# Cross-attention with a scan: features dealt four to a partition, and two steps of the order written later

## The chip, the cores and the metric

The kernel runs on one core of one Trainium2 chip. The time is what the device takes for one execution, in microseconds (us); of several runs the median is given. Every figure of the profile comes from one profiled execution of the kernel.

## The reference

For one sequence of T = 4096 queries and S2 = 3202 context rows, both with H = 512 features, all in float32 (the batch is 1; `input_ids` is not used):

```python
x = layernorm(builder_state, g1, beta1)          # 4096 x 512
base_n = layernorm(base_state, g1, beta1)        # 3202 x 512
q, k, v = heads(x, Wq, bq), heads(base_n, Wk, bk), heads(base_n, Wv, bv)   # 8 heads of 64
attn = softmax(q @ k.T / sqrt(64))
x = builder_state + (attn @ v) @ W_o.T + b_o
xn = layernorm(x, g2, beta2)
U = (xn @ W_in.T + b_in) @ Bmat                  # 4096 x 64
def step(s, u_t):                                # one after the other over t
    s = silu(s @ A.T) + u_t
    return (s, s)
states = scan(step, 0, U)
out = x + states @ Cmat + (program_probs.mean(axis=1) @ W_prog.T + b_prog)
```

## The kernel before

**Three parts.** Up to about 215 us the context is normalised in chunks, transposed by TensorE, and multiplied by Wk and Wv; both results are stored in device memory (`kd`, `vd`). From there to about 1960 us runs the attention. What is left then, the end of the scan, the last rows and the output, is written at the end.

**The attention.** The queries go in 8 blocks of 512. A block has 4 pairs of heads and each pair 2 halves of 256 queries, which makes 8 units. A unit has 13 steps over the keys. A step is `scores` on TensorE (L635, two score tiles that take turns), `weights` on ScalarE (L705, the exponential) and `product` on TensorE (L745). The weights of a unit are summed step by step (`add`, L713): on VectorE (DVE), and for steps 2, 6 and 10 on GpSimd (POOL). At the unit's end GpSimd adds the two halves of the sum (`fold`, L720), TensorE sums over the partitions (`sums`, L763, tile pd), ScalarE copies the denominators (L797), VectorE inverts and scales, and `fall` (L807) keeps a sum of them. The keys and values of each step are loaded on SyncE's queue (L1098, L1106).

**Between the steps** of a block stand two other chains.

- `queries`, for the block that comes next, in two halves of 256 rows: x is loaded (L880), VectorE takes each row's mean and variance (`stats`, L845), GpSimd makes from them a factor and a shift in three small operations (`factors`, L849 to L851), and ScalarE applies them (`scaled`, L857). VectorE transposes 32 by 32 (`flip`, L932), and SyncE issues 16 DMAs a half (`move`, L944), which bring the 32 by 32 blocks to their partitions, in the tile xn with the features across the partitions. From it TensorE makes the queries of each pair of heads (`heads`, L312).
- `project`, for a block that is done: the residual rows xr are loaded (L978), GpSimd adds the output bias (`row`, L981), TensorE multiplies the attention's output by Wo (`outs`, L987, tile pa), VectorE adds the two (`x1`, L1000), GpSimd adds the last term (`mod`, L1004), and the rows are stored for the end (L1007). The same rows are normalised, flipped and moved as above, and TensorE makes the scan's inputs of them (`inputs`, L1042, tile pu), which ScalarE stores (`kept`, L1051).

The first block's queries, those of the last block and the last block's rows are transposed by TensorE instead (L283); the function `mixes(Q)` tells which.

**The order** of the instructions of the attention is written ahead by `Plan` (L71 on): each piece has an engine, a cost in ns, a due time, pieces that it comes after and buffers that it takes. A list scheduler goes through time with these costs and gives each engine that falls free the ready piece with the earliest due time. Due times count in `STEP`s of 2150 ns, one for each key step; d is the time around which a chain is placed. `from_(d)` names the scores of the step at time d, as something to come after. The chip knows nothing of these times: each engine runs its list in order, and waits where a piece needs another engine's.

```python
plan.add((*k, "scaled"), "ACT", 800, partial(scaled_, v, gets[t], t),
         [(*k, "factors")] + ([(*ks[0], "scaled")] if t else []), d + 3 * STEP + t,
         [] if t else ["xh", "xh"], [("fs", (*k, "stats"))] + gives[t : t + 1])
```

**Layout before.** Partition p of xn holds the features p, 128 + p, 256 + p and 384 + p. A move brings to each of its 32 partitions four pieces of 64 elements, which lie apart in xn.

Of the kernel before, what the change touches and what calls it, by code (L numbers as in the profile page):

```python
# [20 lines left out]
P = 128  # L21
# [149 lines left out]
def xattn_ssm_kernel(  # L171
# [49 lines left out]
    g2s = const.tile([P, NC], F32, name="g2s")  # L221
    be2s = const.tile([P, NC], F32, name="be2s")
    bqkv = const.tile([P, 3 * NC], F32, name="bqkv")
    wc = const.tile([P, NC, NS], F32, name="wc")
# [52 lines left out]

    def transposes(pool, tag, xh, n, name):

        name = f"tp_{name}"  # L280
        tp = pool.tile([P, NC, P], F32, tag=tag, name=name) if pool else m_tile([P, NC, P], name)
        for c in range(NC):
            nc.tensor.transpose(  # L283
                tp[:, c, :n], xh[:n, c * P : (c + 1) * P], ident[:n, :n]
            )
        return tp[:, :, :n]
# [15 lines left out]
    def turned(xn, xh, t, name):  # L302

        tp = transposes(None, "m", xh, P, name)
        yield
        nc.scalar.copy(xn[:, :, t * P : (t + 1) * P], tp)

    def heads(Q, hp, xn):

        pq = m_tile([P, 512], f"pq_{Q}_{hp}")  # L310
        for i in range(NC):
            nc.tensor.matmul(  # L312
                pq,
                wq[:, i, hp * P : (hp + 1) * P],
                xn[:, i, :],
                start=(i == 0),
                stop=(i == NC - 1),
            )
# [9 lines left out]
    def first_queries(x0):  # L328

        xn = first_xn["xn"] = xnp.tile([P, NC, QB], F32, tag="xn", name="xn_0")  # L330
        for t in range(NT):
# [30 lines left out]
    def fetch_w(k, queue, part=slice(0, NC)):  # L362
        queue.dma_start(raw[k][:, part], wsrc[:, part, k * H : (k + 1) * H])

    def gain(k, w):
        for i in range(NC):
            nc.vector.tensor_scalar(
                w[:, i, :], raw[k][:, i, :], g1s[:, i : i + 1], None, ALU.mult
            )
# [9 lines left out]
    def shift(k):  # L379

        t = weighted(raw[k], be1s, f"shift_{k}")
        yield
# [16 lines left out]
    def side():  # L399
# [43 lines left out]
        for i in range(NC):  # L443
            nc.tensor.matmul(
                pt[:, i, :NS], wct[:, i * P : (i + 1) * P], twice, start=True, stop=True
            )
# [61 lines left out]
    def norm_chunk(c):  # L508
        if c < NCH:
            xhs[c] = normalize(cxs.pop(c), keys(c), f"c{c}", pool=cin)  # L510

    def turn_chunk(c):
        if c < NCH:
            g, n = c // GC, keys(c)
            if c % GC == 0:
                cts[g] = ctp.tile([P, NC, GC * CK], F32, tag="ct", name=f"ct_{g}")
            o = key0(c) - key0(g * GC)
            copy = nc.vector.tensor_copy if c % 2 else nc.scalar.copy
            copy(cts[g][:, :, o : o + n], transposes(kps, "t", xhs.pop(c), n, f"c{c}"))  # L519

    with tc.manual_schedule():
# [264 lines left out]
    def finish(w, i, d, plan):  # L786
# [22 lines left out]
        def scale(part):  # L809
# [14 lines left out]
        for t, part in enumerate(parts):  # L824
# [4 lines left out]
                     [("rd", ("den", i, 0))])  # L829
        plan.add(("fall", i), "DVE", 340, fall, [("inverse", i, t) for t in range(len(parts))],  # L830
                 d + 9000, [], [("rd", ("den", i, 0))])
# [4 lines left out]

    def norm_pieces(plan, ks, gets, d, after, names, gives):

# [20 lines left out]
        for t, (k, v) in enumerate(zip(ks, vs)):  # L859
            plan.add((*k, "stats"), "DVE", 870, partial(stats_, v, gets[t], names[t]), [after[t]],  # L860
                     d + t, ["fs"])
            plan.add((*k, "factors"), "POOL", 1050, partial(factors_, v), [(*k, "stats")], d + 2000)
            plan.add((*k, "scaled"), "ACT", 800, partial(scaled_, v, gets[t], t),
                     [(*k, "factors")] + ([(*ks[0], "scaled")] if t else []), d + 3 * STEP + t,
                     [] if t else ["xh", "xh"], [("fs", (*k, "stats"))] + gives[t : t + 1])
        return vs

    def queries(plan, Q, d):
# [3 lines left out]
        for half in range(2):  # L872
# [9 lines left out]
            for t in range(2):  # L882
                plan.add((*ks[t], "load"), "SP", 800, partial(load, t),
                         [(*ks[0], "load")] if t else [from_(d - 2 * STEP)], d - 2 * STEP + t, [] if t else ["x"])
            free = ("x", (*ks[0], "load"))
            nv = norm_pieces(plan, ks, [lambda t=t, v=v: v["x"][:, t] for t in range(2)], d,
                             [(*k, "load") for k in ks], [f"x{r}" for r in at],
                             [] if mixes(Q) else [free] * 2)

            def open_(half=half):  # L890
                if half == 0:
                    w["xn"] = xnp.tile([P, NC, QB], F32, tag="xn", name=f"xn_{Q}")

            def move_(a, half=half, v=v, open_=open_):
                if a == 0:
                    open_()
                move(w["xn"][:, :, half * QU : (half + 1) * QU], v["x"], a)

            def turn(half=half, nv=nv, at=at, v=v, open_=open_):
                open_()  # L900
                xn = w["xn"][:, :, half * QU : (half + 1) * QU]
                v["turns"] = [turned(xn, nv[t]["xh"], t, f"x{at[t]}") for t in range(2)]
# [5 lines left out]
            if mixes(Q):  # L908
# [21 lines left out]
    def flip(pair, xh, t):  # L930

        nc.vector.transpose(  # L932
            pair.rearrange("p t h -> p (t h)").rearrange("p (g t r) -> p t g r", t=2, r=TB)[:, t],
            xh.rearrange("p (g r) -> p g r", r=TB),
        )

    def move(xn, pair, a):

        n = 2 * TB
        of = pair[a * TB : (a + 1) * TB].rearrange("p t h -> p (t h)").rearrange(  # L940
            "p (c b k) -> p b c k", b=P // TB, k=n
        )
        for b in range(P // TB):
            nc.sync.dma_start(xn[b * TB : (b + 1) * TB, :, a * n : (a + 1) * n], of[:, b])  # L944

# [19 lines left out]
    def project(plan, Q, halves, d, index):  # L965

        for half in halves:
# [49 lines left out]
            for t in range(2):  # L1017
# [20 lines left out]
            def inputs(w=w, at=at, last=last):  # L1038
                w["pu"] = m_tile([P, P], f"pu_{at[0]}")
                for c in range(NC):  # L1040
                    for t in range(2):
                        nc.tensor.matmul(  # L1042
                            w["pu"][t * NS : (t + 1) * NS], wc[:, c, :],
                            w["xn"][:, t, c, :] if last else mixed(w["xn"][:, c, :], t),
                            start=(c == 0), stop=(c == NC - 1), skip_group_check=True,
# [21 lines left out]
            else:  # L1067
                copied, xn2, after = [], (*ks[0], "move0"), 16

                def move_(a, w=w, at=at):  # L1070
                    if a == 0:
                        w["xn"] = xp_.tile([P, NC, QU], F32, tag="xn2", name=f"xn2_{at[0]}", bufs=1)
                    move(w["xn"], w["x1"], a)
# [5 lines left out]
                for a in range(P // TB):  # L1079
                    plan.add((*ks[0], f"move{a}"), "SP", 2600, partial(move_, a),  # L1080
                             [(*k, "flip") for k in ks] + ([xn2] if a else []), d + (6 + 2 * a) * STEP,
                             [] if a else ["xn2"], [("x1", (*k2, "outs"))])
# [254 lines left out]
    def last_rows(plan, d):  # L1337
# [26 lines left out]
        def turn_(g):  # L1364
            if g:
                tp = v["tp"][g] = sv["pyl"].rearrange("p (c k) -> p c k", c=NC)
                for c in range(NC):
                    nc.tensor.transpose(tp[:, c, :], v["xh"][g][:, c * P : (c + 1) * P], ident)
            else:
# [106 lines left out]
    def unit(plan, i):  # L1476
# [30 lines left out]
        for c in range(NDC):  # L1507
# [25 lines left out]
            if c == 1:  # L1533
                plan.add(("rest", i), "DVE", 700, partial(rest, w), [("add", i, 1), ("extra", first)],
                         d + 1300, [], [("extra", ("extra", first))])
# [103 lines left out]
    def attend():  # L1639
# [31 lines left out]
        def turned_():  # L1671
# [6 lines left out]
            for c in range(NC):  # L1678
                cs = slice(c * P, (c + 1) * P)
                nc.tensor.transpose(banks[0][:, cs], xh[:, cs], ident)  # L1680
            nc.scalar.copy(xn, banks[0].rearrange("p (c k) -> p c k", c=NC))
# [204 lines left out]
```

## Time and profile before

| | |
|---|---|
| Time, median of 3 runs | 2033.97 us (2031.74 to 2038.98) |
| Profiled execution: its time, its span | 2036.71 us, 2034.9 us |
| Mean granted clock of TensorE | 0.988 of full speed |
| Busy: TensorE, its weight loads | 1967.0 us (97%), 1258.4 us (62%) |
| Busy: VectorE, ScalarE, GpSimd | 1210.8 us (60%), 1134.3 us (56%), 796.7 us (39%) |
| DMA | 246,935 packets, 204.28 MB |

PE is TensorE, PEld its weight loads, DVE VectorE, ACT ScalarE, POOL GpSimd, SP SyncE and SPq what it issues. A line such as L635 is one of the kernel before. A row of a timeline gives the start in us, the duration in us, engine, line, operation, the tiles written and read, and the number of instructions that it joins; in brackets stand the idle time before it and what ended that. A row of a table of windows gives the stretch and its length, then busy time and number of instructions for PE, PEld, DVE, ACT and POOL, then TensorE's granted clock as a share of full speed, the share of the DMA engines that was busy, and GB/s. A row of the waits gives who waited for whom, the total in us, how often, and the longest. A row that groups a line's instructions gives their number, the shortest, median and longest duration in ns, and the first and last start.

### The profile page before, as it was taken

The numbers are of one execution on the slowest core, as the hardware profiler recorded it, in microseconds if no ns is written. First come the engines' busy times: TensorE is split into PE (matmuls) and PEld (weight loads), VectorE is DVE, ScalarE is ACT, GpSimd is POOL, SyncE is SP. The second block draws the span as 40 slices with busy tenths as digits, with TensorE's granted clock in tenths as the row PEclk, the third lists the DMA queues.
The fourth block names the chain that finished last, engine by engine and source line by source line (L and its number), as shares of the span: only waits on it lengthen the run. The fifth ranks groups of instructions, "written<-read, shape, count | busy, mean of one in ns | idle before, by whom it ended". The sixth has DMA issues, their size and how long they took to land.

```text
span 2034.9 us, 66527 instructions
## 1 busy us (share of the span) xinstructions
PE 1967.0 (97%) x29070; PEld 1258.4 (62%) x29070; DVE 1210.8 (60%) x1533; ACT 1134.3 (56%) x1478; POOL 796.7 (39%) x631
## 2 busy tenths in 40 slices
PE   8999999999999999999999999999999999989996
PEld 4444566665666666666666566666666666655674
DVE  4321367566766666666656675677556655655585
ACT  2233566665656555555666665656565565654553
POOL 2111234345433453345334643345334533444324
PEclk9999999999999999999999999999999999999998
DMA  5632333223422343224322342233322322544475
GB/s 170 188 102 64 100 95 90 59 80 93 110 71 77 92 110 87 76 69 110 90 63 81 83 108 65 80 105 102 83 77 77 93 75 63 149 139 116 123 201 197
DMA packets 246935, 204.28 MB, mean 100 GB/s; under 512 B 80809, under 2 KB 220073, under 8 KB 246637
## 3 DMA queue, kind: packets, MB, share of 16 engines
q1 hardware_dynamic: 242088, 192.28, 33.4%
q10 hardware_dynamic: 4548, 7.67, 1.3%
q8 instruction: 231, 3.78, 0.8%
q14 instruction: 68, 0.55, 0.1%
HBM read 156.32 MB, written 29.88 MB: 92 GB/s over the span
## 4 chain that ended last, share of the span: by engine, by line
PE 70%; DVE 11%; POOL 9%; issue 3%; SPq 3%; ACT 2%; DMA 2%; DVEq 0%; POOLq 0%; ACTq 0%
PE s L635 24%; PE po L745 24%; DVE acc L713 7%; PE pq L312 5%; POOL acc L713 4%; PE pk L584 4%; PE pv L551 4%; PE pa L987 3%; SPq L944 2%; ACT p L705 1%; PE pd L763 1%; DVE rd L804 1%; DMA x<-in_x_dram 1%; POOL rstd_x L850 1%; DVE acc L699 1%
## 5 line engine op out<-in xcount | busy, mean ns | idle before, releaser
L705 ACT ACTIVATE p<-s,shifts 128x1024 f32<-128x1024 f32 (+1 forms) x832 | 889.1, 1080 | 528.5 <-PE s L635 517.4
L635 PE MATMUL s<-q,k 64*64 64x256 f32 x12800 | 839.8, 379 | 16.7 <-ACT p L705 15.6
L713 DVE TENSOR_TENSOR acc<-p,acc 128x1024 f32<-128x1024 f32 (+1 forms) x515 | 620.2, 1204 | 381.4 <-POOL acc L713 315.7
L745 PE MATMUL po<-p,v 64*64 64x256 f32 x12800 | 825.1, 378 | 0.0
L713 POOL TENSOR_TENSOR acc<-p,acc 128x1024 f32<-128x1024 f32 x189 | 446.7, 2363 | 765.4 <-DVE acc L713 419.6
L635 PEld LDWEIGHTS s<-q,k 64*64 64x64 f32 x12800 | 485.9, 134 | 248.1 <-ACT p L705 36.5
L745 PEld LDWEIGHTS po<-p,v 64*64 64x64 f32 x12800 | 491.4, 134 | 192.8 <-issue 6.1
L720 POOL TENSOR_TENSOR acc<-acc 128x512 f32<-128x512 f32 x64 | 102.1, 1595 | 141.1 <-DVE acc L713 141.1
L713 DVE TENSOR_TENSOR acc<-p,p 128x1024 f32<-128x1024 f32 x64 | 95.9, 1499 | 40.0 <-ACT p L705 34.3
L312 PE MATMUL pq<-xn,wq 128*128 128x512 f32 x256 | 118.3, 605 | 0.0
L804 DVE RECIPROCAL rd<-rd 128x256 f32<-128x256 f32 (+1 forms) x65 | 112.4, 1729 | 2.2
L987 PE MATMUL pa<-wo,o 128*128 128x512 f32 x240 | 107.0, 599 | 0.0
L551 PE MATMUL pv<-wv,ct 128*128 128x512 f32 (+1 forms) x208 | 96.4, 617 | 1.0 <-ACT ct L519 0.7
L584 PE MATMUL pk<-ct,wk 128*128 128x512 f32 (+1 forms) x224 | 88.8, 549 | 0.0
L784 DVE TENSOR_TENSOR o<-po,o 128x256 f32<-128x256 f32 x64 | 27.1, 423 | 95.3 <-ACT o L780 94.8
L312 PEld LDWEIGHTS pq<-xn,wq 128*128 128x128 f32 x256 | 46.0, 189 | 57.5 <-issue 57.5
L321 ACT ACTIVATE q<-pq,bias 128x512 f32<-128x512 f32 x32 | 22.0, 687 | 105.7 <-PE pq L312 105.7
L987 PEld LDWEIGHTS pa<-wo,o 128*128 128x128 f32 x240 | 44.4, 190 | 56.0 <-issue 56.0
L699 DVE TENSOR_TENSOR acc<-x,acc 2x256 f32<-2x256 f32 x128 | 74.9, 585 | 2.9
L519 DVE COPY ct<-tp_c 128x512 f32<-128x512 f32 (+1 forms) x13 | 8.5, 651 | 105.1 <-PE tp_c L283 105.1
L551 PEld LDWEIGHTS pv<-wv,ct 128*128 128x128 f32 (+1 forms) x208 | 38.4, 193 | 44.9 <-issue 42.7
L584 PEld LDWEIGHTS pk<-ct,wk 128*128 128x128 f32 x224 | 39.2, 190 | 42.6 <-issue 42.6
(215 smaller groups left out, 1192.8 us busy)
## 6 DMA issues: line engine op xcount, KB each, us to landing
k<-kd SPq DMA_DIRECT2D x432, 128.0 KB, 2.2
v<-vd SPq DMA_DIRECT2D x432, 128.0 KB, 2.3
xn<-x SPq DMA_DIRECT2D x416, 32.0 KB, 1.9
xr<-in_x_dram SPq DMA_DIRECT2D x30, 256.0 KB, 3.5
x1d<-xr SPq DMA_DIRECT2D x30, 256.0 KB, 2.4
x<-in_x_dram SPq DMA_DIRECT2D x28, 256.0 KB, 3.2
cx<-in_ctx_dram SPq DMA_DIRECT2D x25, 256.0 KB, 3.0
vd<-vs SPq DMA_DIRECT2D x25, 256.0 KB, 2.4
```

The lines of the kernel that those rows point to most:

```text
L312: nc.tensor.matmul(pq, wq[:, i, hp * P : (hp + 1) * P], xn[:, i, :], start=(i == 0), stop=(i == NC - 1),)
L551: nc.tensor.matmul(pv[h * HD : h * HD + n, :H], ct[:, k, o : o + n], wv[:, k, :], start=(i == 0), stop=(i == NC // parts - 1), skip_group_ ...
L584: nc.tensor.matmul(pk[:, :n_g], wk[:, i, hp * P : (hp + 1) * P], ct[:, i, :n_g], start=(i == 0), stop=(i == NC - 1),)
L635: nc.tensor.matmul(s[k0 : k0 + HD, a, b, :], kts[(*w["at"][:2], c)][r, b * CK + k0 : b * CK + k0 + HD], q[r], start=True, stop=True, skip_ ...
L699: nc.vector.tensor_tensor(to[r], t[r], to[r], ALU.add)
L705: nc.scalar.activation(t[:, :, :nb, :], w["ps"][c][:, :, :nb, :], AF.Exp, bias=w["shift"])
L713: engine.tensor_tensor(w["acc"][:, :, :nb, :], t[:, :, :nb, :], before[:, :, :nb, :], ALU.add)
L720: nc.gpsimd.tensor_tensor(acc[:, :, 0, :], acc[:, :, 0, :], acc[:, :, 1, :], ALU.add)
L745: nc.tensor.matmul(w["po"][a * HD : (a + 1) * HD, k, :QU], vts[Q, hp, c][r, b, a * HD : (a + 1) * HD], t[r, a, b, :], start=(c == 0 and b ...
L804: nc.vector.reciprocal(w["rd"][:, part], w["rd"][:, part])
L944: nc.sync.dma_start(xn[b * TB : (b + 1) * TB, :, a * n : (a + 1) * n], of[:, b])
L987: nc.tensor.matmul(v["pa"], o_t[Q, c, half][:, t * P : (t + 1) * P], wo[:, c, :], start=(c == 0), stop=(c == NC - 1),)
```

## The change

**Layout.** Partition p of the turned rows now holds the features 4p to 4p + 3. The flip therefore reads its input with a step of four elements, and so do TensorE's transposes of queries and rows; xn has four pieces of 64 rows, each with all its features together, so that a move brings to each of its 32 partitions one run of 1 KB. There are as many moves as before (416 DMAs). `heads` reads eight runs of 64 elements in place of 512 in a row, `inputs` four runs of 32, a KB apart. The query weights, the gains and shifts that go with queries and rows, and the weights of the scan's inputs are laid out in the same way; for that, four small vectors are loaded in four pieces each, where two vectors had one load each. The context's path keeps its layout.

**Order.** `scaled` also comes after the scores of a later step: 8 steps after d for queries, 18 for rows (not the last block's). `inputs` comes after the scores 30 steps after d (not the last block's). The loads of x and xr may go two steps earlier. Five costs in the plan are changed: fold 1250 to 1620, fall 340 to 410, factors 1050 to 2000, rest (VectorE's addition of the last keys) 700 to 1200, move 2600 to 1300.

In the order that comes out, the tail from the last unit's end on and most steps of each unit are as before; on TensorE 180 of 2894 rows of the order differ.

```diff
@@ transposes, turned
-    def transposes(pool, tag, xh, n, name):
+    def transposes(pool, tag, xh, n, name, of=lambda c: slice(c, None, NC)):
...
-                tp[:, c, :n], xh[:n, c * P : (c + 1) * P], ident[:n, :n]
+                tp[:, c, :n], xh[:n, of(c)], ident[:n, :n]
...
@@ heads
-                xn[:, i, :],
+                xn[:, :, i, :],
...
@@ the context's path
+    def turned_c(xh, n, name):
+        return transposes(kps, "t", xh, n, name, lambda c: slice(c * P, (c + 1) * P))
...
@@ loads at the start
-        for t, src in ((be1s, beta1), (bqkv, b_qkv), (g2s, g2), (be2s, beta2)):
+        for t, src in ((be1s, beta1), (bqkv, b_qkv)):
             nc.sync.dma_start(t, src)
         for c in range(4, 7):
             load_chunk(c)
+        for t, src in ((g1q, g1), (be1q, beta1), (g2s, g2), (be2s, beta2)):
+            for k in range(NC):
+                n = P // NC
+                nc.sync.dma_start(t[k * n : (k + 1) * n], src.rearrange("(p c) k -> k p c", c=NC)[k])
...
@@ finish
-        plan.add(("fold", i), "POOL", 1250, partial(fold, w), [("add", i, NDC - 1)], d + 500)
+        plan.add(("fold", i), "POOL", 1620, partial(fold, w), [("add", i, NDC - 1)], d + 500)
...
@@ norm_pieces
-            plan.add((*k, "factors"), "POOL", 1050, partial(factors_, v), [(*k, "stats")], d + 2000)
+            plan.add((*k, "factors"), "POOL", 2000, partial(factors_, v), [(*k, "stats")], d + 2000)
             plan.add((*k, "scaled"), "ACT", 800, partial(scaled_, v, gets[t], t),
-                     [(*k, "factors")] + ([(*ks[0], "scaled")] if t else []), d + 3 * STEP + t,
+                     [(*k, "factors")] + ([(*ks[0], "scaled")] if t else []) + wait, d + 3 * STEP + t,
...
@@ queries
-                         [(*ks[0], "load")] if t else [from_(d - 2 * STEP)], d - 2 * STEP + t, [] if t else ["x"])
+                         [(*ks[0], "load")] if t else [from_(d - 4 * STEP)], d - 4 * STEP + t, [] if t else ["x"])
...
-                             [] if mixes(Q) else [free] * 2)
+                             [] if mixes(Q) else [free] * 2, [from_(d + 8 * STEP)])
...
-                    plan.add((*ks[0], f"move{a}"), "SP", 2600, partial(move_, a),
+                    plan.add((*ks[0], f"move{a}"), "SP", 1300, partial(move_, a),
...
@@ flip, move
-            pair.rearrange("p t h -> p (t h)").rearrange("p (g t r) -> p t g r", t=2, r=TB)[:, t],
-            xh.rearrange("p (g r) -> p g r", r=TB),
+            pair.rearrange("p t h -> p (t h)").rearrange("p (b c t r) -> p t b c r", b=P // TB, c=NC, t=2)[:, t],
+            xh.rearrange("p (b r c) -> p b c r", b=P // TB, c=NC),
...
-            nc.sync.dma_start(xn[b * TB : (b + 1) * TB, :, a * n : (a + 1) * n], of[:, b])
+            nc.sync.dma_start(xn[b * TB : (b + 1) * TB, a], of[:, b])
...
@@ project
-                         [(*ks[0], "load")] if t else [from_(d - 4 * STEP)], d - 4 * STEP + t, [] if t else ["x"])
+                         [(*ks[0], "load")] if t else [from_(d - 6 * STEP)], d - 6 * STEP + t, [] if t else ["x"])
...
-                             [f"y{r}" for r in at], [("x1", (*k2, "outs"))] * 2 * last)
+                             [f"y{r}" for r in at], [("x1", (*k2, "outs"))] * 2 * last,
+                             [] if last else [from_(d + 18 * STEP)])
...
-                            w["xn"][:, t, c, :] if last else mixed(w["xn"][:, c, :], t),
+                            w["xn"][:, t, c, :] if last else w["xn"][:, :, c, t * TB : (t + 1) * TB],
...
-            plan.add((*k2, "inputs"), "PE", 700, inputs, copied, d + after * STEP - now, ["m"], [("xn2", xn2)])
+            plan.add((*k2, "inputs"), "PE", 700, inputs, copied + ([] if last else [from_(d + 30 * STEP)]),
+                     d + after * STEP - now, ["m"], [("xn2", xn2)])
```

More of the change, by code (lines that the diff above doesn't have):

```diff
@@ L362, in fetch_w @@
     def fetch_w(k, queue, part=slice(0, NC)):
-        queue.dma_start(raw[k][:, part], wsrc[:, part, k * H : (k + 1) * H])
+        of = wsrc if k else wqkv_t.rearrange("(p c) o -> p c o", c=NC)
+        queue.dma_start(raw[k][:, part], of[:, part, k * H : (k + 1) * H])
     def gain(k, w):
@@ L367, in gain @@
             nc.vector.tensor_scalar(
-                w[:, i, :], raw[k][:, i, :], g1s[:, i : i + 1], None, ALU.mult
+                w[:, i, :], raw[k][:, i, :], (g1s if k else g1q)[:, i : i + 1], None, ALU.mult
             )
@@ L379, in shift @@
     def shift(k):
-        t = weighted(raw[k], be1s, f"shift_{k}")
+        t = weighted(raw[k], be1s if k else be1q, f"shift_{k}")
         yield
@@ L444, in side @@
             nc.tensor.matmul(
-                pt[:, i, :NS], wct[:, i * P : (i + 1) * P], twice, start=True, stop=True
+                pt[:, i, :NS], wct[:, i::NC], twice, start=True, stop=True
             )
@@ L518, in turn_chunk @@
             copy = nc.vector.tensor_copy if c % 2 else nc.scalar.copy
[L519 removed]
+            copy(cts[g][:, :, o : o + n], turned_c(xhs.pop(c), n, f"c{c}"))
     with tc.manual_schedule():
@@ L829, in finish @@
                      [("rd", ("den", i, 0))])
-        plan.add(("fall", i), "DVE", 340, fall, [("inverse", i, t) for t in range(len(parts))],
+        plan.add(("fall", i), "DVE", 410, fall, [("inverse", i, t) for t in range(len(parts))],
                  d + 9000, [], [("rd", ("den", i, 0))])
@@ L835, in from_, with norm_pieces @@
         return ("scores", *divmod(min(int(d / STEP), len(steps) - 1), NDC))
-    def norm_pieces(plan, ks, gets, d, after, names, gives):
+    def norm_pieces(plan, ks, gets, d, after, names, gives, wait):
         vs = [{}, {}]
@@ L1079, in project @@
                 for a in range(P // TB):
-                    plan.add((*ks[0], f"move{a}"), "SP", 2600, partial(move_, a),
+                    plan.add((*ks[0], f"move{a}"), "SP", 1300, partial(move_, a),
                              [(*k, "flip") for k in ks] + ([xn2] if a else []), d + (6 + 2 * a) * STEP,
@@ L1533, in unit @@
             if c == 1:
-                plan.add(("rest", i), "DVE", 700, partial(rest, w), [("add", i, 1), ("extra", first)],
+                plan.add(("rest", i), "DVE", 1200, partial(rest, w), [("add", i, 1), ("extra", first)],
                          d + 1300, [], [("extra", ("extra", first))])
```

26 lines of the change are left out of this document (15 added, 11 removed).

## The prediction, before the changed kernel was run

> **What bounds the kernel now.** I read the shares of busy time first, then TensorE's waits, then a table of windows, one for each query block, and last the timelines around each long gap.
>
> ```profile
> PE 1967.0 (97%) x29070; PEld 1258.4 (62%) x29070; DVE 1210.8 (60%) x1533; ACT 1134.3 (56%) x1478; POOL 796.7 (39%) x631
> ...
> 224.00:443.00 219.00, 218.27 (x3745) 146.61 (x3747) 139.64 (x156) 140.18 (x170) 82.95 (x48) 1.00 0.29 81
> 443.00:661.00 218.00, 214.26 (x3475) 139.97 (x3471) 140.51 (x164) 130.61 (x164) 95.39 (x64) 0.99 0.32 87
> ...
> 1754.00:1960.00 206.00, 193.53 (x3108) 134.34 (x3104) 124.67 (x164) 116.11 (x158) 80.62 (x55) 0.98 0.46 132
> ```
>
> TensorE (the first pair in a window: length, then PE busy) is busy 218.27 of 219 us in the first block. No change here takes a matmul away, so only its idle time and its slow stretches can be won. In the second block it idles 3.7 us, in the last (1754 to 1960) 12.5 us. All gaps from 224 to 1960, the changed part, come to 36.4 us. Who ended them:
>
> ```profile
> PE s L635 <- ACT p L705: 15.6, 17, 2.7
> PE pd L763 <- POOL acc L720: 9.8, 4, 6.9
> PE pu L1042 <- DVE x L1000: 4.8, 1, 4.8
> PE pu L1042 <- DMA xn<-x: 4.5, 2, 3.2
> PE tp_x L283 <- ACT u L1051: 1.5, 1, 1.5
> ```
>
> These five rows (total, times, longest) hold 36.2 of it. The clock adds to them:
>
> ```profile
> 503.70:512.00 8.30, 8.22 (x125) 5.58 (x129) 5.26 (x6) 5.04 (x7) 5.32 (x4) 0.79 0.31 70
> 722.60:731.00 8.40, 8.32 (x128) 5.70 (x132) 5.27 (x6) 5.14 (x7) 5.42 (x4) 0.80 0.33 70
> 940.90:950.00 9.10, 9.00 (x140) 6.22 (x144) 5.27 (x6) 5.84 (x8) 6.12 (x4) 0.81 0.29 63
> ...
> 1642.40:1650.00 7.60, 7.55 (x84) 5.13 (x88) 2.02 (x2) 2.82 (x4) 2.35 (x1) 0.60 0.11 32
> 1832.20:1839.00 6.80, 6.77 (x88) 4.04 (x88) 5.75 (x9) 2.62 (x6) 2.36 (x1) 0.71 0.20 52
> 1887.50:1894.00 6.50, 6.42 (x77) 4.27 (x77) 2.33 (x5) 3.67 (x6) 5.83 (x9) 0.75 0.49 152
> ```
>
> Each window starts where a gap ends; the third number from the end is the granted clock. After six of the gaps it is 0.60 to 0.81. Window times missing clock (8.30 x 0.21 and so on) gives 1.74 + 1.68 + 1.73 + 3.04 + 1.97 + 1.63 = 11.8 us. So 36.4 + 11.8 = 48.2 us is all that could be won there.
>
> **Why TensorE waits.** One pattern comes in five blocks:
>
> ```profile
> 503.78 1.09 PE L635 MATMUL s<-q,k 64*64 64x256 f32 x16 [2.71 <-ACT p L705]
> ...
> 941.00 1.17 PE L635 MATMUL s<-q,k 64*64 64x256 f32 x16 [1.93 <-ACT p L705]
> ...
> 1377.60 1.09 PE L635 MATMUL s<-q,k 64*64 64x256 f32 x16 [1.88 <-ACT p L705]
> ...
> 493.58 0.43 SPq L880 DMA_DIRECT2D x<-in_x_dram  x1
> ...
> 496.48 0.69 DVE L845 BATCH_NORM_STATS2 st_x<-x 128x6 f32<-128x512 f32 x1 [3.47 <-DMA x<-in_x_dram]
> ...
> 497.49 1.11 POOL L849 TENSOR_SCALAR rstd_x<-mv_x 128x1 f32<-128x1 f32 x1 [1.96 <-DVE mv_x L846]
> ...
> 500.37 0.94 POOL L851 TENSOR_SCALAR nm_x<-mv_x,rstd_x 128x1 f32<-128x1 f32 x1
> ...
> 494.34 1.11 ACT L705 ACTIVATE p<-s,shifts 128x1024 f32<-128x1024 f32 x1 [0.61 <-PE s L635]
> 496.07 1.11 ACT L705 ACTIVATE p<-s,shifts 128x1024 f32<-128x1024 f32 x1 [0.61 <-PE s L635]
> 501.34 0.81 ACT L857 ACTIVATE xh_x<-x,nm_x,rstd_x 128x512 f32<-128x512 f32 x1 [4.16 <-POOL nm_x L851]
> ```
>
> From below: ScalarE runs in order, and its row normalisation (L857) held it for 4.16 us, with the exponentials queued behind. It waited for GpSimd's three small factor operations, of which the first begins at 497.49 and the last ends at 501.31, 3.8 us where the plan reckons 1.05; those waited for DVE's statistics, and these for x, loaded only at 493.58. Of the five such gaps three are shown; those that end at 723 and 1159 have 2.51 and 1.73 us: 10.8 us in all. After the one at 1378 the clock stays at 1.00, as after the one at 1159.
>
> The last block's two longest gaps are another chain:
>
> ```profile
> 1812.27 0.38 SPq L978 DMA_DIRECT2D xr<-in_x_dram  x1
> ...
> 1832.23 1.13 PE L763 MATMUL pd<-acc,ones 64*64 64x256 f32 x8 [6.92 <-POOL acc L720]
> ...
> 1873.98 0.42 SPq L978 DMA_DIRECT2D xr<-in_x_dram  x1
> 1877.21 1.27 POOL L981 TENSOR_TENSOR xr<-xr,rowb 128x512 f32<-128x512 f32 x1 [12.49 <-DMA xr<-in_x_dram]
> 1887.54 1.76 PE L1042 MATMUL pu<-xn,wc 128*64 128x128 f32 x14 [4.82 <-DVE x L1000]
> ```
>
> The residual rows xr are issued late, on a SyncE queue filled with groups of four moves (four times the 0.6 us of L944's row below); GpSimd waits for them in its own order, 12.49 us in the second case, with additions and the fold behind, and TensorE waits for the fold (6.92) or for x1 (4.82).
>
> **The change, part by part.** In the new order I laid the trace's durations from the end of `outs` (pa) in each block.
>
> *Scaled later, x two steps earlier.* Exponentials follow each other in steps of 1.73 us (494.34, 496.07). With x two steps sooner and the scaling five later than planned, the factors gain 7 x 1.73 = 12 us on it, more than the 4.16 us they were late. Won: 10.8 us, and the clock behind the first three, 1.74 + 1.68 + 1.73 = 5.2 us. What moves with it: two flips and sixteen moves behind each pair of scalings, up to the next block's first heads product. I find 3 to 10 us left there.
>
> *Inputs behind the scores of 30 steps, moves cheaper.* The two waits of pu for moves (1.30 and 3.16 us) go: 4.5 us, and 3.04 us of clock. In the new order the products stand 13 to 20 us after the last landing. The wait behind `kept` (1.5 us) goes too, its transposes now standing after a later product.
>
> *xr two steps earlier, folds and factors costed as they are.* The last two xr loads go out about 10 us earlier and GpSimd's row additions stand clear of the fold. Of the 9.8 us for folds I count 9.0 as gone, 0.7 staying in the first block, whose order there is the same; the 4.82 us goes whole; clock 1.97 + 1.63 = 3.6 us.
>
> *The moves.* Each of 416 carries 32 rows of 1 KB, where it had 128 pieces of 256 B.
>
> ```profile
> L944 SPq DMA_DIRECT2D xn<-x x416: 585/599/1974, 277.2 to 1872.2; - x139
> L1106 SPq DMA_DIRECT2D v<-vd x468: 319/382/1738, 220.2 to 1954.2; - x156
> L312 PE MATMUL pq<-xn,wq x256: 592/592/697, 176.9 to 1742.3; 128*128 128x512 f32 x128
> L1042 PE MATMUL pu<-xn,wc x240: 272/273/477, 496.8 to 1899.0; 128*64 128x128 f32 x120
> L1378 PE MATMUL pu_l<-xn_l,wc x8: 272/272/323, 1986.4 to 1987.2; 128*64 128x128 f32 x8
> L932 DVE STREAM_TRANSPOSE x<-xh_y x28: 667/688/712, 474.6 to 1853.7; 128x512 f32<-128x512 f32 x28
> L470 DVE TENSOR_REDUCE sums<-cb x1: 2889/2889/2889, 89.7 to 89.7; 128x64 f32<-128x1600 f32 x1
> L665 DVE TENSOR_REDUCE m<-sm x32: 677/684/692, 216.3 to 1810.5; 128x1 f32<-128x512 f32 x32
> ```
>
> Their issue (599 ns) should come near the 382 ns of a v load, which has rows of 1 KB; the bounds are 319 and 599. By itself this is worth nothing: SyncE bounds nothing else. At 599 the queue is as full as before, and that I price as a rival.
>
> *Strided reads on TensorE.* The heads products now read eight runs of 64 elements, the inputs four of 32. The inputs already read short runs (32 elements, between two row blocks) and take 273 ns, like the whole rows of L1378 at 272. The 1 ns between them, as a share of 256 x 0.592 us, is 0.6 us: between 0 and 0.6, I take 0.
>
> *Strided reads on DVE.* The flip (688 ns) now gathers each fourth element. The one strided read in the trace, L470 (1600 elements, 2889 ns), is to be compared with a whole row's 684 ns for 512, or 2138 for 1600 in proportion: 1.35 times. Bounds: 0 and, with a fixed start allowed for in L665, 1.6 times, +0.4 us a flip. 52 flips make at most 21 us of an engine that is 60% busy. It counts where a flip pair stands before the last addition of a unit: in blocks 1 to 6 I find the fold of the third unit after `outs` ready 14.7 us after its end and TensorE at its sums at 16.3, so some 1.5 us of slack. With +0.8 us for a pair 0.7 us stays; with factors that take 3.8 us again where I laid 2.0 nothing stays, and a gap of 1.1 us. At L470's ratio and without that, 0. Over five blocks that is 0 to 5.5 us; I take 2.
>
> *Fourteen more small loads in the start.* They stand in SyncE's queue ahead of the next context chunk and the first store of vd, each at about such a store's 0.38 us:
>
> ```profile
> 11.75 1.75 SPq L505 DMA_DIRECT2D cx<-in_ctx_dram  x4
> 16.72 0.38 SPq L565 DMA_DIRECT2D vd<-vs  x1
> ```
>
> 14 x 0.38 = 5.3 us, of which the pause from 13.50 to 16.72 covers 3.2. The other 2.1 delay a store and a later chunk that has time. Between 0 and 2.1, I take 0.5.
>
> **The sum.** Gaps won: 10.8 + 4.5 + 1.5 + 9.0 + 4.8 = 30.6. Clock: 5.2 + 3.0 + 3.6 = 11.8. Given back: 2.0 + 0.5. So 39.9 us from 2036.7, the profiled execution's own time, is 1996.8. That execution is 2.7 us above the median; by the median it would be 1994. I say 1996. Some 6 us of small gaps stay, most of them 0.4 us after `outs` and before a block's end.
>
> [...]
>
> **Rivals.**
>
> *B, the fold waits instead.* Flips and factors both at their upper prices put the fold 1.1 us behind TensorE, and each such gap may bring 1.7 us of slow clock, as after the one of 1.93 us: in six blocks 6 x (1.1 + 1.7) = 17 instead of the 2 taken, so 2012 by the profiled time. For it: the slack is the smallest that I found. Against: the flips' own row is the nearer evidence for a short price. 0.12.
>
> *C, the moves get no cheaper and the postponed chain is late.* If a move stays at 599 ns, sixteen take 3.5 us more than I laid, the 3 us before the next block's heads product go, and six blocks wait up to 4 us with 1.7 of clock: 34 us back, so about 2031. Against: v's 382 ns. 0.08.
>
> *D, slower: the stride of 16 bytes is dear on DVE.* It decides from the point where the stall of a flip pair passes the gain: 40 us over 26 pairs is 1.5 us, after 1.5 us of slack if every pair has that, so 3.0 us a pair, a flip at 2.2 us, 3.2 times the present. At four times (2.75 us) a pair costs 4.1, stalls 2.6 and loses 1.7 of clock: 26 x 4.3 = 112, so about 2109. At 3.5 times, 1.9 a pair, near 2047. Against it stands L470 at 1.35 to 1.6; but L470 steps 256 bytes through another operation, and no flip in the trace reads with a step. [...] 0.12.
>
> **How the numbers follow.** The forecast A has 0.68, with its own range 1986 (all 48.2 won, by the median) to 2003 (by the profiled time, with 5.5 at the folds, 2.1 in the start, 0.6 on TensorE). A and B together are 0.80 and set the range: 1986 to 2018, which is B with its gaps at 2 us each. About 0.3%, 6 us, is what a measurement of this kernel can tell from no change. Faster: A and B, 0.80; same: C, 0.08; slower: D, 0.12.
>
> **What would show it.** Right: TensorE's waits without x1, without xn and with under 5 us for exponentials; granted clock 1.00 in every window from 443 to 1950; PE busy some 10 us less, by the clock; moves near 0.38 us; flips at 0.7 to 1.1 us. Wrong: a row of TensorE waiting for folds over 7 us, or for heads products' inputs; L312 above 600 ns; flips above 2 us.

## The result, and the profile after

The changed kernel takes 2017.24 us (median of 5 runs, 2016.16 to 2018.0) where the kernel before took 2032.97 (5 runs, 2031.34 to 2038.98): 0.9918 of it, with an interval of 0.9902 to 0.9934. It is 0.8% faster, and the time lies in the range, but 16 us were won where 38 were forecast. The profiled execution of the changed kernel took 2018.0 us, with a span of 2016.0.

The line of the engines' shares and TensorE's waits, as before (who waits for whom, total us, times, longest). Lines are numbered by the changed kernel: 649 are the scores (635 before), 777 the sums (763), 1056 the inputs (1042), 734 the fold, 1013 x1, 994 row, 957 the moves.

```profile
PE 1965.9 (98%) x29070; PEld 1261.4 (63%) x29070; DVE 1277.6 (63%) x1533; ACT 1131.9 (56%) x1478; POOL 791.7 (39%) x631
...
PE pd L777 <- DVE x L1013: 10.2, 10, 1.8
...
PE pd L777 <- POOL acc L734: 6.1, 7, 3.0
...
PE s L649 <- ACT p L719: 2.5, 6, 0.4
...
PE pu L1056 <- DVE x L1013: 0.4, 1, 0.4
```

The waits that were to go did go: exponentials 15.6 to 2.5 us, pu for moves 4.5 to none, pu for x1 4.8 to 0.4. A new first row stands there: the sums' tile pd waits for x1, ten times. The sums take two buffers of a pair that `outs` holds until VectorE has made x1 of it.

The windows of two blocks, and two of the five of 8 us behind the new gaps (third number from the end: granted clock):

```profile
443.00:661.00 218.00, 214.52 (x3472) 140.02 (x3468) 152.27 (x164) 130.43 (x164) 94.39 (x64) 0.99 0.30 87
...
1754.00:1940.00 186.00, 184.33 (x3004) 129.67 (x3000) 122.14 (x156) 112.27 (x155) 76.30 (x54) 1.00 0.47 140
```

```profile
519.00:527.00 8.00, 6.97 (x90) 4.42 (x93) 7.09 (x10) 2.48 (x6) 6.91 (x9) 0.79 0.36 108
...
1393.00:1401.00 8.00, 6.51 (x81) 4.15 (x85) 6.93 (x9) 3.08 (x7) 6.79 (x9) 0.79 0.45 144
```

The last block idles 1.7 us, where it had idled 12.5. The blocks before it idle about as much as they did (3.5 us in the second; 3.7 before), and in five of them the clock is at 0.79 for 8 us, 8 x 0.21 = 1.7 us each. (Within the first of these windows it is 0.50 from 521.7 to 525.0.)

Why x1 is late, in the second block, from timelines of SyncE's queue, GpSimd, VectorE and TensorE:

```profile
489.51 3.44 SPq L957 DMA_DIRECT2D xn<-x  x4
492.99 0.58 SPq L991 DMA_DIRECT2D xr<-in_x_dram  x1
...
496.08 1.28 POOL L994 TENSOR_TENSOR xr<-xr,rowb 128x512 f32<-128x512 f32 x1 [8.51 <-DMA xr<-in_x_dram]
497.79 1.28 POOL L994 TENSOR_TENSOR xr<-xr,rowb 128x512 f32<-128x512 f32 x1 [0.43 <-DMA xr<-in_x_dram]
499.02 2.37 POOL L727 TENSOR_TENSOR acc<-p,acc 128x1024 f32<-128x1024 f32 x1
...
501.42 3.88 DVE L727 TENSOR_TENSOR acc<-p,acc 128x1024 f32<-128x1024 f32 x3 [6.48 <-POOL acc L727]
...
518.38 0.68 DVE L1013 TENSOR_TENSOR x<-pa,xr 128x512 f32<-128x512 f32 x1
...
519.21 0.61 PE L777 MATMUL pd<-acc,ones 64*64 64x256 f32 x2 [1.77 <-DVE x L1013]
520.64 0.44 PE L777 MATMUL pd<-acc,ones 64*64 64x256 f32 x3 [0.81 <-DVE x L1013]
```

From above: the fourth group of moves of the first half's rows is issued from 489.51, and only then the second half's residual rows xr. GpSimd waits 8.51 us for them, with an addition of weights behind. VectorE waits 6.48 us for that addition, then works off its backlog with x1 last. TensorE's sums wait 1.77 us for the first x1 and 0.81 for the second.

In the kernel before, the same place of the same block looks like this, with the waits for xr of its GpSimd, and then those of the changed kernel's:

```profile
494.05 0.90 SPq L978 DMA_DIRECT2D xr<-in_x_dram  x2
...
493.16 2.37 POOL L713 TENSOR_TENSOR acc<-p,acc 128x1024 f32<-128x1024 f32 x1 [6.78 <-DVE acc L713]
...
501.27 2.49 POOL L981 TENSOR_TENSOR xr<-xr,rowb 128x512 f32<-128x512 f32 x2
...
POOL xr L981 <- DMA xr<-in_x_dram: 26.0, 4, 12.5
...
POOL xr L994 <- DMA xr<-in_x_dram: 57.6, 12, 8.8
```

There xr was issued no earlier, and behind sixteen moves too. But the addition of weights (493.16) stood ahead of `row` (501.27) in GpSimd's list, and GpSimd waited for xr in the last block alone. So the new thing is less that xr is late than that `row` now stands ahead of that addition.

What the new layout did to single instructions (shortest, median, longest in ns, then first and last start):

```profile
L957 SPq DMA_DIRECT2D xn<-x x416: 507/589/1795, 289.3 to 1854.6; - x139
...
L946 DVE STREAM_TRANSPOSE x<-xh_y x28: 1071/1120/1171, 476.9 to 1841.2; 128x512 f32<-128x512 f32 x28
...
L318 PE MATMUL pq<-xn,wq x256: 592/592/697, 177.7 to 1738.5; 128*128 128x512 f32 x128
...
L285 PEld LDWEIGHTS tp_x<-ident,xh_x x32: 195/211/217, 117.2 to 1657.3; 128*128 128x128 f32 x32
```

A move is issued in 589 ns, hardly less than before (599), though it has a quarter of the pieces. A flip takes 1120 ns, 1.63 times its 688. The heads products are unchanged; the weight load of TensorE's transposes takes 211 ns where it took 141.

### The profile page after: what moved, and what is told of

It reads as the page before. It is cut to its first block, busy times and chain, and to the rows that moved or that the text cites. A ratio compares the mean times of both kernels' runs of the same rounds, so it can differ in the third digit from the quotient of the medians.

```text
span 2016.0 us, 66547 instructions
## 1 busy us (share of the span) xinstructions
PE 1965.9 (98%) x29070; PEld 1261.4 (63%) x29070; DVE 1277.6 (63%) x1533; ACT 1131.9 (56%) x1478; POOL 791.7 (39%) x631
## 4 chain that ended last, share of the span: by engine, by line
PE 91%; DVE 3%; POOL 2%; issue 1%; DMA 1%; ACT 1%; SPq 0%; DVEq 0%; ACTq 0%; POOLq 0%
PE po L759 33%; PE s L649 33%; PE pq L318 6%; PE pa L1000 5%; PE pk L598 4%; PE pv L565 4%; PE pd L777 2%; DVE acc L727 1%; PE pu L1056 1%; PE sm L667 1%; PE po L747 1%; ACT p L719 1%; POOL acc L734 1%; PE tp_c L285 1%; DMA xr<-in_x_dram 0%
## 5 line engine op out<-in xcount | busy, mean ns | idle before, releaser
L759 PE MATMUL po<-p,v 64*64 64x256 f32 x12800 | 834.1, 378 | 0.4 <-DVE o L798 0.4
L727 POOL TENSOR_TENSOR acc<-p,acc 128x1024 f32<-128x1024 f32 x189 | 460.7, 2437 | 706.0 <-DVE acc L727 380.0
L649 PEld LDWEIGHTS s<-q,k 64*64 64x64 f32 x12800 | 490.9, 133 | 229.2 <-ACT p L719 24.6
L734 POOL TENSOR_TENSOR acc<-acc 128x512 f32<-128x512 f32 x64 | 89.7, 1401 | 116.4 <-DVE acc L727 114.2
L727 DVE TENSOR_TENSOR acc<-p,p 128x1024 f32<-128x1024 f32 x64 | 100.6, 1572 | 48.4 <-ACT p L719 42.8
L713 DVE TENSOR_TENSOR acc<-x,acc 2x256 f32<-2x256 f32 x128 | 97.6, 762 | 2.9
L994 POOL TENSOR_TENSOR xr<-xr,rowb 128x512 f32<-128x512 f32 x30 | 45.9, 1544 | 57.6 <-DMA xr<-in_x_dram 57.6
```

The costliest lines, as they stand in the source:

```text
L649: nc.tensor.matmul(s[k0 : k0 + HD, a, b, :], kts[(*w["at"][:2], c)][r, b * CK + k0 : b * CK + k0 + HD], q[r], start=True, stop=True, skip_ ...
L713: nc.vector.tensor_tensor(to[r], t[r], to[r], ALU.add)
L727: engine.tensor_tensor(w["acc"][:, :, :nb, :], t[:, :, :nb, :], before[:, :, :nb, :], ALU.add)
L734: nc.gpsimd.tensor_tensor(acc[:, :, 0, :], acc[:, :, 0, :], acc[:, :, 1, :], ALU.add)
L759: nc.tensor.matmul(w["po"][a * HD : (a + 1) * HD, k, :QU], vts[Q, hp, c][r, b, a * HD : (a + 1) * HD], t[r, a, b, :], start=(c == 0 and b ...
L994: nc.gpsimd.tensor_tensor(v["x"], v["x"], rowb, ALU.add)
```

## The experiments

Two theories were set against each other. **Theory 1**: xr comes late, because moves are as dear as ever and stand ahead of it; GpSimd waits in its order, and x1 is late. **Theory 2**: the longer flips fill VectorE and make x1 late by themselves. The kernel before takes 2028 to 2030 us on the chips used here, so each time is given as a ratio to the kernel before on the same chip.

### GpSimd's row additions later

```diff
-                plan.add((*ks[t], "row"), "POOL", 1300, partial(row, vs[t]), [(*ks[t], "load")], d - STEP)
+                plan.add((*ks[t], "row"), "POOL", 1300, partial(row, vs[t]),
+                         [(*ks[t], "load")] + ([] if last else [from_(d - -6 * STEP)]), d - STEP)
```

> The changed kernel, but GpSimd's addition of the bias to the residual rows (row) also comes after the scores that stand 6 steps behind d, so that it stands behind one more addition of weights (step 6 of the unit) in GpSimd's list; layout, moves, loads and all other pieces stay where they are. Theory 1 (the second half's xr load stands behind sixteen moves that take 0.59 us each and not the planned 0.33; GpSimd waits 8.5 us for it with additions behind, VectorE's additions and x1 come late, and pd waits for x1): the ten waits of pd for x1 (10.2 us) and the slow clock behind them (5 x 1.7 us) go, so 1998 to 2003. Theory 2 (the flips, 1.13 us where they were 0.69, fill VectorE and make x1 late by themselves): pd still waits for x1, 2013 to 2018.

Measured: 2009.61 us, 0.9913 of before (0.9887 to 0.9939). Once more, on another chip, to be compared with the old layout:

> The changed kernel with GpSimd's row additions later, once more, beside the same with the old layout: 0.989 to 0.994 of before. The new layout is dearer by the long flips (folds and x1 late by 0.5 to 0.9 us in a block), so 3 to 9 us slower than order_row_late_again.

Measured: 2009.94 us (2009.66 to 2010.5), 0.9904 (0.9877 to 0.9930). The changed kernel itself, on that second chip:

> The changed kernel once more, beside the others on one chip. Theory 1 and 2 alike: 0.99 of the kernel before, as measured (0.9902 to 0.9934); pd waits for x1 about twice a block.

Measured: 2014.31 us (2012.99 to 2017.41), 0.9930 (0.9911 to 0.9950). Its sums wait ten times for x1 again, 9.1 us in all, but the clock behind these waits is another. Windows of 8 us from these waits on, in the second and in the fifth block:

```profile
517.00:525.00 8.00, 6.71 (x112) 4.03 (x108) 7.09 (x10) 4.21 (x7) 6.49 (x9) 1.00 0.63 186
...
1172.00:1180.00 8.00, 6.32 (x58) 3.58 (x62) 6.63 (x10) 2.31 (x6) 6.60 (x9) 0.59 0.33 102
```

Of the five pairs of waits, four are followed by the full clock here, with first waits of 0.47, 0.59, 1.12 and 1.15 us, and only the one of 1.71 us by a slow one; the changed kernel's first execution had slow clock behind all five, after 0.86 and 0.91 us too. The waits of row_late, a window behind the place of the first gap, and its GpSimd timeline:

```profile
PE sm L686 <- DVE m L679: 4.4, 5, 0.9
...
PE pd L777 <- DVE x L1013: 3.9, 5, 0.8
...
516.00:524.00 8.00, 7.21 (x124) 4.59 (x120) 7.10 (x10) 4.21 (x7) 6.41 (x9) 1.00 0.66 196
...
494.90 2.37 POOL L727 TENSOR_TENSOR acc<-p,acc 128x1024 f32<-128x1024 f32 x1 [7.48 <-DVE acc L727]
497.24 3.49 POOL L994 TENSOR_TENSOR xr<-xr,rowb 128x512 f32<-128x512 f32 x2
```

The addition of weights starts at 494.90 in place of 499.02, and GpSimd waits for xr nowhere in this block. The waits for x1 fall from 10.2 to 3.9 us, and the clock stays at 1.00, in all five blocks and in both runs. So `row` ahead of the addition, waiting for xr, is what cost the long waits. That it also cost slow clock fits all these profiles: with `row` later there is none at the five places, with `row` early there is some at five, at one and (in order_only, below) at three of them. How much of it one execution meets is not settled by the waits.

In time less came than theory 1 expected: 14 to 19 us were to be won, and by the ratios it is 1 to 5 (4.4 between the two medians on the second chip, whose runs do not overlap). VectorE's backlog does not go wholly: a wait of 0.8 us for x1 stays in each of five blocks, and one of 0.9 us for VectorE's maximum m, TensorE's sm, comes behind it. That one comes in after_again too, in the four blocks with the full clock, so slow clock and waits for m partly stand in for each other.

### The order alone, the layout alone

The old layout with every change of the order; and the new layout with the plan of before.

> The new order (planned costs, waits for later scores, earlier loads) on the layout of before: flips at about 0.69 us, moves of 256-byte pieces. Theory 1: the moves take about as long as with the new layout, xr is as late, GpSimd waits 8 us again, and pd waits for x1; VectorE has 0.9 us less to do before x1, so the gaps shrink by at most 1 us each: 2008 to 2017. Theory 2: the waits of pd for x1 go with the long flips: 1998 to 2003.

Measured: 2014.85 us, 0.9941 (0.9922 to 0.9960).

```profile
PE pd L763 <- DVE x L1000: 9.4, 10, 1.6
...
492.28 1.28 POOL L981 TENSOR_TENSOR xr<-xr,rowb 128x512 f32<-128x512 f32 x1 [7.63 <-DMA xr<-in_x_dram]
```

With short flips GpSimd waits 7.63 us for xr and pd waits 9.4 us for x1, hardly less than the 10.2. Theory 2 falls as the cause of these waits. Over 8 us behind its five pairs of waits the clock is 0.79 three times and 1.00 twice.

> The new layout with the order of before (planned costs, waits and loads as before). Theory 1: the layout alone wins nothing, because a move's issue stays near 0.59 us; exponentials behind row normalisations and late xr as before: 2030 to 2042. Theory 2: the longer flips make folds and x1 late in this order too: 2040 to 2060. Had the moves become as cheap as a v load, SyncE's late loads would come 3 us earlier and the last two long gaps would go: below 2022.

Measured: 2037.73 us, 1.0053 (1.0036 to 1.0070): the layout alone makes the kernel slower. Its moves, its waits, one of its gaps, and the window behind that:

```profile
L957 SPq DMA_DIRECT2D xn<-x x416: 507/588/1916, 277.7 to 1868.8; - x139
...
PE s L649 <- ACT p L719: 15.7, 22, 2.9
...
1159.74 1.09 PE L649 MATMUL s<-q,k 64*64 64x256 f32 x16 [2.92 <-ACT p L719]
...
1159.70:1167.70 8.00, 7.34 (x136) 5.05 (x140) 5.80 (x7) 6.28 (x9) 5.02 (x4) 1.00 0.25 68
```

The exponentials wait as before, and order_only has about the ratio of the changed kernel (0.9941 beside 0.9918 and 0.9930), so the whole gain is the order's, and in this order the medians show no price of the layout. What makes layout_only slower by some 9 us I have not followed. A gap of 2.92 us is followed by the full clock here, where 1.93 us were followed by 0.81 in the kernel before.

### The moves' planned cost back at 2600

```diff
-                    plan.add((*ks[0], f"move{a}"), "SP", 1300, partial(move_, a),
+                    plan.add((*ks[0], f"move{a}"), "SP", 2600, partial(move_, a),
```

(The same in both places, queries and rows.)

> The changed kernel, but the plan reckons a group of four moves at 2600 ns again (1300 in the change; measured 2400). Theory 1: the plan then knows that xr comes late and puts GpSimd's row addition 2.5 steps later in the list, still ahead of the addition of step 6; the wait there shrinks, and the gaps of pd for x1 get smaller or go: 2000 to 2010. Theory 2: no change, 2013 to 2018.

Measured: 2031.08 us, 1.0011 (0.9999 to 1.0024). A miss for both theories.

```profile
PE pd L777 <- DVE x L1013: 9.5, 10, 1.5
...
PE pu L1056 <- DMA xn<-x: 5.7, 5, 2.1
...
496.26 2.51 POOL L994 TENSOR_TENSOR xr<-xr,rowb 128x512 f32<-128x512 f32 x2 [8.61 <-DMA xr<-in_x_dram]
```

GpSimd's row still stands ahead of the same addition, and waits 8.61 us as before: the place in the list counted here, not the planned time. With the true cost the planner also puts more loads of k and v between the groups of moves (in the third block eight behind the first three groups, where the changed kernel has five), and pu waits for moves again. Of the rest, 8 us lie behind the last scores (1956.5 to 2029.8, where the changed kernel has 1950.6 to 2016.0); what set that part back I have not followed.

### What a move costs, by itself

> The changed kernel with 32 DMAs more at its start on SyncE's queue, eight of each kind: SBUF to SBUF 32 rows of 1 KB, the same with each row in four pieces of 256 bytes, SBUF to SBUF 128 rows of 1 KB, and device memory to SBUF 32 rows of 1 KB (they write a tile that nothing reads). If a move's issue goes by the number of pieces: the first kind 0.32 to 0.40 us, the second 0.6. If it goes by both ends lying in SBUF: the first three 0.55 to 0.65, the last 0.3 to 0.4. If the main loop's moves are held up by something else: the first two both under 0.45.

Of these runs' times only the instructions matter. In the order of the expectation:

```profile
L295 SPq DMA_DIRECT2D pr_a<-pr_src x8: 507/588/628, 2.2 to 10.4; - x8
...
L297 SPq DMA_DIRECT2D pr_b<-pr_src x8: 599/600/677, 11.0 to 15.5; - x8
...
L302 SPq DMA_DIRECT2D pr_c<-pr_src x8: 598/599/600, 16.2 to 20.7; - x8
...
L304 SPq DMA_DIRECT2D pr_d<-in_x_dram x8: 419/419/586, 21.3 to 24.8; - x8
```

Between two places in SBUF a transfer was issued in 588 to 600 ns (medians), with 32 pieces of 1 KB, 128 of 256 B or 128 of 1 KB. From device memory the same 32 rows took 419. The change cut the number of pieces, and in these rows the price does not go by it. What it goes by is not wholly told by the two ends: the start's small loads of gains and shifts (L547 of the changed kernel, 128 pieces of 4 bytes) come from device memory and take 597 to 598 ns as well.

### The costs alone; the waits taken away one by one

The kernel before with the five planned costs alone (fold, fall, factors, rest, move):

> The kernel before with the five planned costs of the change alone: no waits for later scores, no earlier loads, old layout. If the waits of exponentials behind row normalisations are won by the postponed scaled: TensorE's row for ScalarE's weights stays at 10 us or more, and the time at 0.993 to 1.003 of before. If the costs alone put the pieces right: 0.985 to 0.992.

Measured: 2063.47 us, 1.0173 (1.0152 to 1.0193), outside both expectations.

```profile
PE po L745 <- DVE o L784: 37.3, 6, 7.0
...
PE s L635 <- ACT p L705: 5.8, 8, 3.3
...
541.42 0.69 DVE L845 BATCH_NORM_STATS2 st_x<-x 128x6 f32<-128x512 f32 x1 [7.02 <-DMA x<-in_x_dram]
```

Fewer exponentials wait (5.8 us). GpSimd waits for xr in every block from the second on here (6.48 us in the second), so these costs alone already put `row` ahead of the addition. And VectorE's statistics stand in its list 7.02 us before x has landed, with `join` behind; the next unit's products need the buffer that `join` reads, and wait up to 7.0 us. An engine is held by a late load once more.

The changed kernel without the two waits of `scaled`, and without the wait of `inputs`:

> The changed kernel without the two waits of scaled for a later step's scores; everything else of the change stays. By the prediction's step (the postponed scaled is what frees the exponentials): TensorE's row for ScalarE's weights back at 8 us or more, 0.995 to 1.002 of before. By what costs_only showed (the honest cost of the factors already frees them, and the waits serve to keep the other pieces in place): that row stays under 7 us, products wait for VectorE's join (4 us or more, several times), 1.000 to 1.020 of before.

Measured: 2048.35 us, 1.0088 (1.0060 to 1.0116).

```profile
PE s L649 <- ACT p L719: 15.5, 22, 2.1
PE po L759 <- DVE o L798: 11.9, 6, 2.1
```

The exponentials' waits are back at 15.5 us in all, as the prediction's step has it, but in 22 waits of at most 2.1 us instead of 17 of up to 2.7; and products wait for `join` too, though for 2 us and not 4. Both halves of the expectation hold in part.

> The changed kernel without the wait of inputs for the scores 30 steps behind d; everything else stays. If that wait is what took the waits of pu for moves away: they come back, 1 to 4 us in several blocks, 0.994 to 1.000 of before. If it is not needed: no row of pu for xn over 1 us, 0.991 to 0.995 as the changed kernel.

Measured: 2025.68 us, 0.9979 (0.9961 to 0.9996).

```profile
PE pu L1056 <- DMA xn<-x: 14.1, 6, 6.7
```

pu waits for moves six times, 14.1 us in all. That wait is what took them away, and more of them than the 4.5 us in the kernel before.

### The order and the later row additions, on the old layout

The new order and the later row additions, on the layout of before:

> The new order on the layout of before, with GpSimd's row additions behind the scores that stand 6 steps behind d. Theory 1 (late xr is what costs, long flips cost a little): row_late's time less its short fold waits and part of its x1 waits, so 0.984 to 0.990 of the kernel before. A rival, that the new layout helps in the new order: slower than row_late, above 0.992.

Measured: 2003.22 us, 0.9875 (0.9855 to 0.9895).

> The new order with the later row additions on the old layout, once more: 0.985 to 0.990 of before.

Measured: 2004.31 us (2000.47 to 2005.55), 0.9878 (0.9851 to 0.9905), beside row_late_again's 2009.94 on the same chip: the layout costs 5.6 us in this order, and this is the fastest of all versions.

```profile
PE s L635 <- ACT p L705: 4.5, 7, 2.0
...
PE pd L763 <- DVE x L1000: 3.1, 5, 0.8
...
PE pd L763 <- POOL acc L720: 1.7, 3, 0.8
```

The folds' short waits, 0.47 to 0.65 us in each of six blocks of the changed kernel, are gone but for three, 1.7 us in all where row_late has 4.0, and those for x1 are 3.1 us where row_late has 3.9.

## Why the prediction was right or wrong

*What bounds the kernel* was right: TensorE, and only its gaps and slow stretches could be won.

*Scaled later, x two steps earlier*: the 10.8 us were won. ScalarE's row normalisations wait for the factors once, 1.6 us, where they waited 44.6 us before, and no_scaled_wait brings waits of the exponentials back, though mostly short ones. *Inputs behind 30 steps*: won, and no_inputs_wait brings back more. *The last block's xr*: won, both long gaps are gone.

*The row additions of blocks 2 to 7* are the step that failed: the prediction follows `row` in the last block alone, and puts its waits at nothing everywhere else without a reason. The new order has `row` ahead of an addition of weights in each of these blocks, and GpSimd waits there for xr, 8 us a block. That costs TensorE the ten waits for x1, and in the seventh block a wait of 3.0 us for a fold, behind a wait of GpSimd of 6.89 us for xr; order_only has that one too (4.2 us), and row_late does not:

```profile
1604.83 0.66 PE L777 MATMUL pd<-acc,ones 64*64 64x256 f32 x8 [3.00 <-POOL acc L734]
```

*The moves* failed with it. I expected 382 ns from a load of v, and it was 589; a load from device memory was the wrong row to go by for a move between two places in SBUF. Rival C said that the moves might get no cheaper, but looked for the damage at the next block's heads products. They never waited. The damage was at xr, in the same queue. Had the sixteen moves ahead of it taken 382 ns each instead of 589, xr would have come 3.3 us sooner, or 5.8 against the 11.9 us that they took in the second block with their pauses; GpSimd would have waited some 3 to 5 us for it instead of 8.5. That is an estimate from these rows: no run has a cheap move, and how much of the loss is the price and how much the place of `row` stays open.

*The clock* was mis-sized. I took 11.8 us as won for good. The old gaps' losses are gone, but five new places lose 1.7 us each, 8.6 us together. And the loss after a gap is not a fixed price: layout_only keeps the full clock after 2.92 us, and after_again loses clock behind one of the five places only. It also differs between executions of the kernel before, which on the other two chips take 2023 us with a mean clock of 0.993 and 2036 with 0.988. The profiled execution had 0.988, so it was one with much slow clock, and to take all of the 11.8 us off the median as well ("1994") was wrong: the median execution has less of it to give.

*Strided reads on DVE* came at the upper bound, +0.43 us a flip (688 to 1120 ns). The fixed start in that bound is an estimate: by two reductions of the kernel before, 684 ns for 512 elements (L665) and 411 for 256 (L807), it is about 0.14 us, and with it L470 took 1.57 times as long as by their rate. The 2.0 us given back were about right here: the folds' six short waits make 3.1 us, where I had left 0.7 + 2.0. But the price of the layout depends on the order: nothing to be seen between order_only and the changed kernel, 5.6 us between order_row_late_again and row_late_again. Rival B had the mechanism, the fold, with 1.1 us a block and slow clock; it was 0.5 and none. Rival D's point, 2.2 us a flip, was not reached (1.12). *Strided reads on TensorE*: no change in products, as said (592 ns for the heads products in both); I had not counted the transposes' weight loads, 141 to 211 ns. *The start*: the first scores at 217.9 in place of 217.2, 0.7 us for the 0.5 forecast, by luck in part, since a small load took 0.60 us and not 0.38.

The sum, profiled execution against profiled execution: forecast 1996.8, measured 2018.0, so 21.2 us short. Of that, 10.2 are pd's waits for x1, 3.0 the seventh block's fold, 8.6 the clock behind the waits for x1, 0.4 the short waits of folds (3.1 less 2.7), and 2.3 are to be taken off, since the small waits for exponentials fell from 4.8 to 2.5. That makes 19.9; the other 1.3 us I can't place. In after_again there is less slow clock, and waits for m (3.6 us) stand in its place. Nor was xr all that stood between this kernel and 1996: with `row` later, waits for m (4.4 us), exponentials (4.4), folds (4.0) and x1 (3.9) remain.

## What to carry to other kernels

In lists that engines serve in order, moving a step later moves its loads and transfers too: follow each queue that they pass, in every block and not only where the old wait was, with prices of transfers between the same kinds of memory (a move within SBUF was issued in 589 ns, a load of v in 382). Setting a single planned cost right need not help: in moves_2600 `row` kept its place in the list, and GpSimd waited 8.61 us there as before. A loss of clock read from one execution is not a price (the changed kernel lost clock behind its waits for x1 at five places in one, and at one place in another): run the kernel again before it goes into a sum. Before a layout is changed to make a transfer's pieces larger, measure whether its price depends on the pieces at all (here 588 to 600 ns in each case), and price the strided reads that it brings elsewhere (here flips of 1120 ns in place of 688).

## What the runs showed of the hardware

- In move_price the issue price of a transfer within SBUF did not go by number or size of pieces (medians of 588 to 600 ns over a factor of four in both).
- A step of 16 bytes made VectorE's 32 by 32 transpose 1.63 times as long (688 to 1120 ns) and TensorE's weight load 1.5 times (141 to 211 ns). No run has these two operations with another step, so what another costs is not shown.
- In the changed kernel's profiled execution the clock loses 1.7 us at a time (0.79 over 8 us), after 1.77 + 0.81 us idle and after 0.91 + 0.81 us alike, each time with 0.61 us of matmuls between the two gaps. In after_again, the same kernel, it loses nothing after 1.15 + 0.81 us, and in layout_only nothing after 2.92 us: the length of a gap does not settle it. What decides between a slow and a full clock after the same gaps no run here shows.
